# Two attention layers on one core: value batches sized to the score group, and softmax sums of layer 0 merged before they are summed over partitions

## The chip, the cores and the metric

The kernel runs on one core of a Trainium2 chip, in one launch. The metric is the device time of a run in microseconds; less is better. The core's engines run side by side and wait for each other through semaphores: TensorE (PE in the profile, its weight loads PEld), VectorE (DVE), ScalarE (ACT), GpSimd (POOL) and SyncE (SP, which issues transfers here).

## What is computed

The input x has 8 images of 64 channels and 64x64 positions, in 32-bit floats. Two self-attentions over the 4096 positions of each image follow each other:

```python
# layer 0
f = Wf @ x; g = Wg @ x            # 8 channels each
h = Wh @ x                        # 64 channels
beta = softmax(f.T @ g, axis=2)   # 4096 x 4096 for each image
x = x + h @ beta.T
# layer 1
xn = group_norm(x)                # 8 groups
q, k, v = split(w_qkv @ xn)       # 64 channels each
attn = softmax(q.T @ k / 8)
x = x + w_proj @ (attn @ v)
```

The kernel takes no maximum out of the softmax: it computes exponentials of the scores, the values weighted by them, and the sums of the exponentials, and multiplies by the reciprocal sums at the end. A general path for inputs whose sums leave a safe range stands behind a branch and isn't run here.

## The kernel before

An image's positions are kept as two halves of 2048 side by side on the partitions (64 channels of each half). The queries are worked on in 4 chunks of 512 columns of both halves (`NC`, `CW`), and for each chunk the keys in 16 steps t of 128 positions from each half p (`NT`). One *block* of scores in layer 0 is 128 keys by 512 queries: for one t there are four, (p, h) with p the half of the keys and h that of the queries. One block fills one PSUM bank. Images and layers follow each other as layer 0 of image 0, layer 0 of image 1, layer 1 of image 0, layer 0 of image 2, layer 1 of image 1 and so on. So there is one first stretch of layer 0 with two images (8 chunks) and six later ones of 4 chunks, each between stretches of layer 1.

TensorE's instructions are kept in the order in which the program makes them (`in_order`); those of the other engines are placed by a scheduler, within what `issue_after` says. All TensorE matmuls go through one helper, L137.

In a stretch of layer 0 the loop at L748 makes one *group* at a time. Eight PSUM banks are there: 1 to 6 for scores or lent to other work in pairs, and 0 and 7 (`outer`) as accumulators of the values, of which the one that is free at the moment takes a seventh block of scores. The group so has

- 7 blocks when the second accumulator is free (`closed == 0`) and no work wants it (`taken != BANK`),
- 6 otherwise,
- and 2 fewer when a pair of banks is lent (`taken == PAIR`) to a projection, a values product or the like, which `take` gives out by due steps.

After the group's scores, `scalar.activation` at L776 makes the exponentials, up to four banks at a time, into tiles `e` that hold the four blocks of one t (128x2048 floats; six such tiles, `ppool`). Then `ended` makes the due work and the *batch* of values: `weigh` multiplies values by finished exponentials of earlier groups into an accumulator (`acc`). `due_part` (L629) takes the batch from the list `ready`, whose entries are the two blocks of one (t, p). It counts in half blocks of the batch, 256 of an entry's 512 columns being one, so that an entry counts two, and takes up to 7 of them whatever the group holds; an entry that doesn't fit whole is cut in the middle. Blocks and half blocks balance, since one block of scores gives one half block to weigh.

For each t, VectorE adds the e tile into the chunk's `esum` (L662, 128x2048): esum has four parts, (p, h). At the chunk's end `finish` (L303) makes the rest in pieces with due steps: `sums` multiplies by ones, which adds over the partitions (four products, each in its own 32 columns of the array and its own 32 rows of the result), ScalarE copies the result to `zs`, four small transfers deal it over partitions as `zt`, `reciprocals` inverts it and sends it round through DRAM as `r`, and `result` multiplies the weighted values (`raw`) by it and adds the residual.

In layer 1 `finish` first merges the two p parts of esum on VectorE (L312, 128x1024), and the ones products take 256 columns each. In layer 0 there is no merge: the ones products take 512 columns each, one for every (h, p), and the two p parts are added later as 128x8 numbers (L345).

Of the kernel before, what the change touches and what calls it, by code (L numbers as in the profile page):

```python
# [9 lines left out]
F32 = mybir.dt.float32  # L10
# [9 lines left out]
CW = 512  # L20
P = 128
# [47 lines left out]
def fast_path(  # L69
# [19 lines left out]
    nc = tc.nc  # L89
    B, C, N = x.shape  # L90
# [11 lines left out]
    work = ctx.enter_context(tc.tile_pool(name="work", bufs=2))  # L102
    small = ctx.enter_context(tc.tile_pool(name="small", bufs=2))
# [89 lines left out]
    ones = const.tile([P, C], F32, name="ones")  # L193
# [18 lines left out]
    QP = 2 * CW // P  # L212
# [64 lines left out]
    class Attention:  # L277
# [25 lines left out]
        def finish(self, acc, esum, c, index):  # L303

            n = f"{self.name}_{c}"
            raw = work.tile([P, CW], F32, tag="raw", bufs=4, name=f"raw_{n}")
            copied = self.total(raw, acc)
            zt = small.tile([P, 2, QP], F32, tag="zt", bufs=5, name=f"zt_{n}")
            width = CW if self.kind == 0 else CW // 2
            if self.kind == 1:  # L310
                with tc.issue_after(copied.ins):
                    nc.vector.tensor_add(esum[:, 0], esum[:, 0], esum[:, 1])  # L312
            r = None

            def sums(spare):

                if spare is not None:
                    z = banks[:, spare, :]
                else:
                    z = pair()[:, 0, :]  # L320

                zs = work.tile([P, CW], F32, tag="zs", bufs=1, name=f"zs_{n}")[:, 0:width]
                for h in range(2):
                    for i in range(2):
                        row = 32 * (2 * h + i)
                        what = esum[:, i, h, :] if self.kind == 0 else esum[:, 0, h, ts(i, width)]
                        matmul(
                            z[row : row + 32, 0:width], ones[:, 0:32], what,
                            start=True, stop=True, tile_position=(0, row),
                        )  # L330
                nc.scalar.copy(zs, z[:, 0:width])  # L331
                for h in range(2):
                    for i in range(2):
                        row = 32 * (2 * h + i)
                        dst = zt[ts(h, C), i, :] if self.kind == 0 else zt[row : row + 32, 0, :]
                        nc.sync.dma_start(dst, zs[row : row + 1, :])

            def broadcast():
                nonlocal r
                r = work.tile([P, CW], F32, tag="r", name=f"r_{n}")  # L340

            def reciprocals():
                zh = zt[:, 0, :]
                if self.kind == 0:
                    nc.vector.tensor_add(zh, zh, zt[:, 1, :])  # L345
                rt = stash[:, ts(index, QP)]
                nc.vector.reciprocal(rt, zh)
                broadcast()
                dealt = recips[index]
                nc.sync.dma_start(dealt, rt)  # L350
                for h in range(2):
                    row = dealt[ts(h, C), :].rearrange("p e -> (p e)")
                    nc.sync.dma_start(r[ts(h, C), :], row.partition_broadcast(C))

            def at_once():

                broadcast()
                z = pair()[:, 0, :]
                for h in range(2):
                    matmul(z[ts(h, C), :], ones, esum[:, 0, h, :], start=True, stop=True)  # L360
                nc.vector.reciprocal(r, z)  # L361
                result()
                bounds(r, 1)

            def result():
                nc.vector.tensor_mul(raw, raw, r)  # L366
                self.residual(raw, c)

            if index == 2 * B * NC - 1:
                return (at_once,)  # L370
            return sums, reciprocals, result
# [219 lines left out]
    PAIR, BANK = 1, 2  # L591
# [33 lines left out]
    ready = []  # L625
    acc = esum = first = None
    added = None

    def due_part(ready):  # L629


        room, now_, left = 7, [], []
        for k, j, e, cols in ready:
            size = (cols.stop - cols.start) // (CW // 2)
            if seq[k][0].kind == 1 or room >= size:
                now_.append((k, j, e, cols))
                room -= size
            elif room == 1 and 0 < j < 2 * NT - 1:
                mid = (cols.start + cols.stop) // 2
                now_.append((k, j, e, slice(cols.start, mid)))  # L640
                left.append((k, j, e, slice(mid, cols.stop)))
                room = 0
            else:
                left.append((k, j, e, cols))
                room = 0
        return now_, left
# [60 lines left out]
    closed = 1  # L707
# [14 lines left out]
    while i < len(seq):  # L722
        at, c = seq[i]
        if at.kind == 1:
            for j in range(0, 2 * NT, 2):
                now = i * NT + j // 2
                due, taken = take(now)
                batch, left = ready, []
                t = j // 2
                new = []  # L730
                both_ps = [pair(), pair()]
                for p in range(2):
                    at.scores(both_ps[p], t, p, c)
                e = ppool.tile([P, 2, 2, CW], F32, tag="e", name=f"e_{at.name}_{c}_{t}")
                for p in range(2):
                    nc.scalar.activation(e[:, p], both_ps[p], AF.Exp, scale=at.scale)  # L736
                    new.append((i, j + p, e, slice(0, CW)))
                ended()
            i += 1
            continue  # L740

        last = next(k for k in range(i, len(seq) + 1) if k == len(seq) or seq[k][0].kind == 1)
        units = [
            (k, t, p, h)
            for k in range(i, last) for t in range(NT) for p in range(2) for h in range(2)
        ]
        u = 0
        while u < len(units):  # L748
            k, t = units[u][:2]
            now = k * NT + t  # L750
            due, taken = take(now + 1)
            batch, left = due_part(ready)
            free = outer[1]
            if batch:
                free = outer[(batch[-1][0] + 1) % 2]
                if seq[batch[-1][0]][0].kind == 1 or any(b[1] == 0 for b in batch):
                    closed = max(closed, 1)
            room = list(range(1, 7))
            if closed == 0 and taken != BANK:
                room = sorted(room + [free])  # L760
            if taken == PAIR:
                lent = 0 if room[-1] == 7 else 2
                room = [r for r in room if r not in (2 * lent + 1, 2 * lent + 2)]
            group = list(zip(units[u : u + len(room)], room))
            u += len(group)
            for (k, t, p, h), bank in group:
                seq[k][0].scores(banks[:, bank, :], t, p, h, seq[k][1])
            new = []
            while group:
                (k, t, p, h), bank = group[0]  # L770
                first_ = 2 * p + h
                n_ = min(4 - first_, len(group))
                at, c = seq[k]
                if first_ == 0:
                    e = ppool.tile([P, 2, 2, CW], F32, tag="e", name=f"e_{at.name}_{c}_{t}")
                nc.scalar.activation(  # L776
                    e.rearrange("k p h n -> k (p h) n")[:, first_ : first_ + n_, :],
                    banks[:, bank : bank + n_, :], AF.Exp, scale=at.scale,
                )
                new += [  # L780
                    (k, 2 * t + p, e, slice(0, CW)) for (k, t, p, h), _ in group[:n_] if h == 1
                ]
                group = group[n_:]
            ended()
            lent = None
        i = last
# [5 lines left out]
    bad_ps = banks[0:1, 0, 0:1]  # L792

    def bounds(recip, i):
        ok = work.tile(list(recip.shape), F32, tag="zs", bufs=1, name=f"ok_{i}")
        nc.vector.tensor_scalar(ok, recip, 1.0 / SUM_MAX, None, op0=ALU.is_ge)
        nc.vector.scalar_tensor_tensor(
            ok, recip, 1.0 / SUM_MIN, ok, op0=ALU.is_le, op1=ALU.mult
        )
        least = small.tile([P, 1], F32, tag="least", name=f"least_{i}")  # L800
        nc.vector.tensor_reduce(least, ok, axis=AX.X, op=ALU.min)
        nc.vector.tensor_scalar(bad[:, i : i + 1], least, -1.0, 1.0, op0=ALU.mult, op1=ALU.add)
# [395 lines left out]
```

## Time and profile before

| | |
|---|---|
| median time of 3 runs | 3106.06 us (3105.13 to 3106.15) |
| span of the profiled execution | 3104.1 us |
| TensorE, matmuls busy | 3063.5 us (99%) |
| VectorE busy | 2506.6 us (81%) |
| ScalarE busy | 2045.5 us (66%) |
| first stretch of layer 0 | 23 to 343 us |
| a later stretch of layer 0 | 958 to 1106 us |
| a stretch of layer 1 | 1106 to 1340 us |

The table's last three rows are from the times of the exponentials in the timeline. A matmul of 32-bit floats is two records in the trace (two for each product of values and of ones), one of scores in layer 0 is one record. In the timeline `fg_l` (or `kq_l` with 32*128) are layer 0's scores, `e_l,vt_l` (or `e_l,v_l` with 128*64) its batches, and `esum_l,ones` the ones products; the second number of a row is the time from its first record's start to its last one's end, so what a group occupies is better read from its start to the next group's start. A batch of six half blocks is 12 records of 512 columns; those that are cut have some of 256.

### The profile page before, as it was taken

How to read it: one execution, taken by the hardware profiler on the slowest of the kernel's cores; microseconds unless marked ns; L12 is line 12 of the kernel's file. 1: busy time of each engine (PE TensorE's matmuls, PEld its weight loads, DVE VectorE, ACT ScalarE, POOL GpSimd, SP SyncE). 2: the span in 40 equal slices, each digit the busy share in tenths (PEclk: the TensorE clock that was granted, in tenths of full speed). 3: DMA queues.
4: the chain of work that ended last, by engine and by line, in shares of the span. 5: the costliest groups of instructions: out<-in, count | busy, mean ns of one | idle time of the engine just before them, and what ended most of it. 6: DMA issues, size and time to landing. Idle time of an engine off the chain costs nothing.

```text
span 3104.1 us, 58905 instructions
## 1 busy us (share of the span) xinstructions
PE 3063.5 (99%) x25863; PEld 1122.5 (36%) x25863; DVE 2506.6 (81%) x1616; ACT 2045.5 (66%) x1976; POOL 16.7 (1%) x41
## 2 busy tenths in 40 slices
PE   7999999999999999999999999999999999999998
PEld 2333334333343333433334333343334333334433
DVE  6999876898768987689877997779977799776666
ACT  5788655786557865578555785558855587555554
POOL 2000000000000000000000000000000000000000
PEclk9999999999999999999999999999999999999999
DMA  3000010100101001010011000100001000000000
GB/s 84 22 8 11 18 39 15 32 1 15 39 21 26 1 15 39 22 25 1 15 39 25 21 1 19 42 19 21 1 25 35 19 8 2 14 22 15 10 13 12
DMA packets 61816, 63.16 MB, mean 20 GB/s; under 512 B 34944, under 2 KB 35024, under 8 KB 61552
## 3 DMA queue, kind: packets, MB, share of 16 engines
q1 hardware_dynamic: 60432, 59.16, 7.8%
q8 instruction: 204, 3.34, 0.5%
q14 instruction: 60, 0.49, 0.1%
q0 software_dynamic: 800, 0.15, 0.0%
q10 hardware_dynamic: 320, 0.01, 0.0%
HBM read 25.06 MB, written 8.65 MB: 11 GB/s over the span
## 4 chain that ended last, share of the span: by engine, by line
PE 96%; DVE 1%; ACT 1%; issue 1%; SPq 0%; DMA 0%; ACTq 0%; DVEq 0%
PE banks L137 96%; DVE esum_l L662 1%; ACT e_l L776 1%; SPq L432 0%; ACT e_l L736 0%; DMA w<-in_WgT_dram 0%; DMA x<-in_x_dram 0%; DVE vt_l L298 0%; DVE r_l L361 0%; DVE high_l L422 0%; DMA fg_l<-high_l 0%; ACTq L169 0%; DVE raw_l L366 0%; DVE esum_l L312 0%; ACT full_l L417 0%
## 5 line engine op out<-in xcount | busy, mean ns | idle before, releaser
L662 DVE TENSOR_TENSOR esum_l<-esum_l,e_l 128x2048 f32<-128x2048 f32 x896 | 2052.4, 2291 | 473.2 <-ACT e_l L736 414.5
L736 ACT ACTIVATE e_l<-banks 128x1024 f32<-128x1024 f32 x1024 | 992.8, 1021 | 802.8 <-PE banks L137 770.1
L137 PE MATMUL banks<-e_l,v_l 64*64 64x512 f32 (+1 forms) x8744 | 1098.5, 589 | 0.0
L776 ACT ACTIVATE e_l<-banks 128x2048 f32<-128x2048 f32 (+3 forms) x768 | 955.7, 1310 | 213.1 <-PE banks L137 207.9
L137 PE MATMUL banks<-kq_l 64*64 64x512 f32 (+1 forms) x8448 | 1010.2, 586 | 1.2 <-ACT e_l L776 1.1
L137 PE MATMUL banks<-e_l,vt_l 128*64 128x512 f32 (+1 forms) x3884 | 831.5, 567 | 0.0
L137 PEld LDWEIGHTS banks<-e_l,v_l 64*64 64x64 f32 (+1 forms) x8744 | 360.0, 133 | 576.0 <-issue 534.0
L137 PEld LDWEIGHTS banks<-kq_l 64*64 64x64 f32 (+1 forms) x8448 | 348.7, 134 | 579.3 <-issue 544.6
L137 PEld LDWEIGHTS banks<-e_l,vt_l 128*64 128x64 f32 x3884 | 254.3, 136 | 470.4 <-issue 457.0
L137 PE MATMUL banks<-fg_l 32*128 32x512 f32 x1792 | 220.2, 465 | 10.7 <-ACT e_l L776 5.7
L662 DVE TENSOR_TENSOR esum_l<-e_l,e_l 128x2048 f32<-128x2048 f32 x64 | 146.5, 2288 | 48.4 <-ACT e_l L736 35.9
L137 PEld LDWEIGHTS banks<-fg_l 32*128 32x128 f32 x1792 | 92.1, 183 | 219.4 <-ACT e_l L776 134.8
L137 PE MATMUL banks<-esum_l,ones 128*32 128x512 f32 (+2 forms) x508 | 55.2, 501 | 4.4 <-DVE esum_l L312 2.7
L568 DVE COPY raw_l<-banks 128x512 f32<-128x512 f32 x32 | 22.1, 692 | 31.3 <-PE banks L137 31.3
L366 DVE TENSOR_TENSOR raw_l<-raw_l,r_l 128x512 f32<-128x512 f32 x64 | 43.8, 684 | 0.0
L542 ACT ACTIVATE kq_l<-banks,qkb 128x512 f32<-128x512 f32 x64 | 40.6, 696 | 0.0
L312 DVE TENSOR_TENSOR esum_l<-esum_l 128x1024 f32<-128x1024 f32 x32 | 38.9, 1216 | 0.0
L137 PE MATMUL banks<-xn_l,wqk 64*64 64x512 f32 x256 | 33.4, 592 | 0.0
L331 ACT COPY zs_l<-banks 128x512 f32<-128x512 f32 (+1 forms) x63 | 30.9, 491 | 0.0
L137 PE MATMUL banks<-x,wfg 64*64 64x512 f32 x128 | 19.0, 640 | 9.7 <-DVE low L179 9.3
L137 PEld LDWEIGHTS banks<-wh,x 64*64 64x64 f32 x1024 | 22.0, 135 | 15.7 <-issue 13.3
L137 PEld LDWEIGHTS banks<-wvp,xn_l 64*64 64x64 f32 x1024 | 20.6, 134 | 16.8 <-issue 16.8
(89 smaller groups left out, 378.2 us busy)
## 6 DMA issues: line engine op xcount, KB each, us to landing
r_l<-recips SPq DMA_DIRECT2D x126, 128.0 KB, 2.9
fg_l<-high_l SPq DMA_DIRECT2D x224, 64.0 KB, 2.0
x<-in_x_dram SPq DMA_DIRECT2D x32, 256.0 KB, 5.2
kq_l<-kq_l SPq DMA_DIRECT2D x64, 128.0 KB, 2.3
out_dram<-raw_l SPq DMA_DIRECT2D x64, 128.0 KB, 2.4
kq_l<-high_l SPq DMA_DIRECT2D x32, 64.0 KB, 2.0
zt_l<-zs_l SPq DMA_DIRECT2D x128, 2.0 KB, 1.8
zt_l<-zs_l SPq DMA_DIRECT2D x124, 1.0 KB, 1.7
```

The lines of the kernel that those rows point to most:

```text
L137: in_order(nc.tensor.matmul(*args, **kwargs))
L312: nc.vector.tensor_add(esum[:, 0], esum[:, 0], esum[:, 1])
L331: nc.scalar.copy(zs, z[:, 0:width])
L366: nc.vector.tensor_mul(raw, raw, r)
L542: nc.scalar.activation(self.parts[:, h, cols], ps[:, h, :], AF.Identity, bias=k1["qkb"][:, h : h + 1],)
L568: nc.vector.tensor_copy(raw, acc[0])
L662: added = nc.vector.tensor_add(esum, first if t == 1 else esum, e).ins
L736: nc.scalar.activation(e[:, p], both_ps[p], AF.Exp, scale=at.scale)
L776: nc.scalar.activation(e.rearrange("k p h n -> k (p h) n")[:, first_ : first_ + n_, :], banks[:, bank : bank + n_, :], AF.Exp, scale=at.scale,
```

## The change

Three things are changed.

1. The size of a batch of values in layer 0 follows the size of the score group it stands behind: 7, 6, or two fewer, by the same conditions. It is meant to keep TensorE's and ScalarE's work per group in step, since ScalarE has as many blocks to exponentiate as the group holds while TensorE weighs the batch.
2. In layer 0, too, VectorE merges the two p parts of esum once per chunk, right after the chunk's last add.
3. With merged sums, the ones products of layer 0 take 256 columns in place of 512, the copy to `zs` is half as wide, and the small add in `reciprocals` goes. The buffers are changed to fit: `zs` has two, `zt` four of half the size, and the tile of the bounds check at the end moves from the buffer of `zs` to those of `raw`.

```diff
-            zt = small.tile([P, 2, QP], F32, tag="zt", bufs=5, name=f"zt_{n}")
-            width = CW if self.kind == 0 else CW // 2
-            if self.kind == 1:
-                with tc.issue_after(copied.ins):
-                    nc.vector.tensor_add(esum[:, 0], esum[:, 0], esum[:, 1])
+            zt = small.tile([P, QP], F32, tag="zt", bufs=4, name=f"zt_{n}")
+            width = CW // 2
+            with tc.issue_after(copied.ins if self.kind == 1 else added):
+                nc.vector.tensor_add(esum[:, 0], esum[:, 0], esum[:, 1])
...
-                zs = work.tile([P, CW], F32, tag="zs", bufs=1, name=f"zs_{n}")[:, 0:width]
+                zs = work.tile([P, width], F32, tag="zs", name=f"zs_{n}")
...
-                        what = esum[:, i, h, :] if self.kind == 0 else esum[:, 0, h, ts(i, width)]
                         matmul(
-                            z[row : row + 32, 0:width], ones[:, 0:32], what,
+                            z[row : row + 32, 0:width], ones[:, 0:32], esum[:, 0, h, ts(i, width)],
...
-                        dst = zt[ts(h, C), i, :] if self.kind == 0 else zt[row : row + 32, 0, :]
-                        nc.sync.dma_start(dst, zs[row : row + 1, :])
+                        nc.sync.dma_start(zt[row : row + 32, :], zs[row : row + 1, :])
...
-                zh = zt[:, 0, :]
-                if self.kind == 0:
-                    nc.vector.tensor_add(zh, zh, zt[:, 1, :])
                 rt = stash[:, ts(index, QP)]
-                nc.vector.reciprocal(rt, zh)
+                nc.vector.reciprocal(rt, zt)
...
-    def due_part(ready):
+    def due_part(ready, room):
-        room, now_, left = 7, [], []
+        now_, left = [], []
...
-            batch, left = due_part(ready)
+            wide = 7 if closed == 0 and taken != BANK else 6
+            batch, left = due_part(ready, wide - (2 if taken == PAIR else 0))
...
-        ok = work.tile(list(recip.shape), F32, tag="zs", bufs=1, name=f"ok_{i}")
+        ok = work.tile(list(recip.shape), F32, tag="raw", bufs=4, name=f"ok_{i}")
```

## The prediction

> **What bounds the kernel now.** I read the page's busy shares first, then the chain that ended last, then the costliest groups with shapes kept apart, then the timeline of TensorE and of VectorE in one layer 0 stretch.
>
> The page's first part and the start of its fourth:
>
> ```profile
> PE 3063.5 (99%) x25863; PEld 1122.5 (36%) x25863; DVE 2506.6 (81%) x1616; ACT 2045.5 (66%) x1976; POOL 16.7 (1%) x41
> ...
> PE 96%; DVE 1%; ACT 1%; issue 1%; SPq 0%; DMA 0%; ACTq 0%; DVEq 0%
> ```
>
> TensorE is the bound: matmuls are 96% of the chain. But "99% busy" doesn't say that it streams at its pace; that is read from start to start in TensorE's timeline, here around one chunk boundary of the second layer 0 stretch (columns: start us, us, engine, line, operation, count):
>
> ```profile
> 586.78 0.64 PE L137 MATMUL banks<-esum_l,ones 128*32 128x256 f32 x8
> 587.35 2.79 PE L137 MATMUL banks<-e_l,vt_l 128*64 128x512 f32 x12
> ...
> 627.90 1.06 PE L137 MATMUL banks<-esum_l,ones 128*32 128x512 f32 x8
> 628.90 3.23 PE L137 MATMUL banks<-e_l,vt_l 128*64 128x256 f32 x16
> 632.05 0.73 PE L137 MATMUL banks<-fg_l 32*128 32x512 f32 x6
> 632.72 2.80 PE L137 MATMUL banks<-e_l,vt_l 128*64 128x512 f32 x12
> 635.44 0.74 PE L137 MATMUL banks<-fg_l 32*128 32x512 f32 x7
> 636.11 2.79 PE L137 MATMUL banks<-e_l,vt_l 128*64 128x512 f32 x12
> 638.84 0.98 PE L137 MATMUL banks<-fg_l 32*128 32x512 f32 x7
> 639.75 3.23 PE L137 MATMUL banks<-e_l,vt_l 128*64 128x512 f32 x16
> 642.91 0.73 PE L137 MATMUL banks<-fg_l 32*128 32x512 f32 x7
> ```
>
> Three things are to be seen. The ones products of 512 columns occupy 628.90 - 627.90 = 1.00 us, those of 256 columns 587.35 - 586.78 = 0.57. A batch of six half blocks takes 635.44 - 632.72 = 2.72, of seven 642.91 - 639.75 = 3.16, also where it is cut into 256-column pieces (628.90 to 632.05 = 3.15), so cutting costs nothing. And seven scores take 0.67 (635.44 to 636.11) unless seven scores and a batch of only six stand before them: then 0.91 (638.84 to 639.75).
>
> That last 0.24 us is a wait for ScalarE: seven blocks need one 2048-column exponential and one of 1536, 1876 + 1453 ns = 3.33 us, while TensorE comes back to the same PSUM banks after 2.72 + 0.67. With a batch of seven it comes back after 3.83 and waits for nothing.
>
> VectorE is the second engine to watch, since layer 0 loads it fully. The groups with shapes kept apart:
>
> ```profile
> L662 DVE TENSOR_TENSOR esum_l<-esum_l,e_l 128x2048 f32<-128x2048 f32 x896 | 2052.4, 2291 | 473.2 <-ACT e_l L736 414.5 <-ACT e_l L776 16.1 <-DVE esum_l L662 0.9
> L312 DVE TENSOR_TENSOR esum_l<-esum_l 128x1024 f32<-128x1024 f32 x32 | 38.9, 1216 | 0.0
> ```
>
> VectorE's timeline (start us, us), and the second chunk of the third stretch by engine (length, then busy us of TensorE, its weight loads, VectorE and ScalarE):
>
> ```profile
> 987.98 11.87 DVE L662 TENSOR_TENSOR esum_l<-esum_l,e_l 128x2048 f32<-128x2048 f32 x5
> ...
> 993.00:1030.00 37.00, 37.00 (x217) 12.45 (x215) 35.55 (x16) 30.97 (x29) 0.00 (x0) 1.00 0.06 14
> ```
>
> Only 16.1 us of the adds' idle time is for layer 0's exponentials (L776). Five dependent adds take 11.87, so they start (11.87 - 2.29) / 4 = 2.395 apart; fifteen per chunk are 35.9 us, and a chunk lasts 37.
>
> **What the Trainium skill says.** "Perfetto Trace Analysis", Identifying the Most-Contended Engine, warns that matmul occupancy is a poor measure; the trace agrees, since the 0.24 us waits lie inside the 99%. "VectorE: DVE Perf Modes", The TRN2 errata, gives an fp32 tensor add as (N+151)/0.96 ns: 2291 for 2048 elements and 1224 for 1024; the trace has 2291 and 1216, and I use the trace. "TensorE: Matmul & The Clock Gate", Back-to-back issue gap, has a stream cost in proportion to its columns; the trace agrees in the difference, 1.00 - 0.57 = 0.43 us for half the columns.
>
> **The change part by part.** Counts for the changed kernel are those of its built order of instructions; it has 828 score or layer 1 groups and 828 batches, as before, so no overhead of a group is added.
>
> 1. *Ones products of 256 columns.* 32 chunks x 0.427 us (finer starts: 0.996 - 0.569) = 13.7 us off TensorE. It is on the bound everywhere, in layer 1 too, where the last chunk of each image's layer 0 has its products. The copy of sums on ScalarE falls from 595 to 383 ns, beside TensorE.
>
> 2. *Batches matched to the group.* The work is the same; only waits go. In the timeline before, seven scores after (seven scores, six half blocks) occur 46 times and cost 11.9 us over their 0.665, smaller batches between large groups in the first stretch cost another 5. Over 0.66 per group, a later layer 0 stretch (six of them, some 150 us each) loses 2.60: 0.67 on entering from layer 1, and eight waits of 0.20 to 0.29. In the built order three of those eight are left per stretch, with the entry: 0.67 + 0.21 + 0.25 + 0.29 = 1.42. Saved 1.2 x 6 = 7.1. The first stretch (two images, 20 to 345 us) loses 11.1, of which I find some 3.9 still there (start-up, and two groups of five after S7 V6): 7.2 saved. Where a projection or a values copy shares the group, five scores and five half blocks stand against 1876 + 601 ns of exponentials and 0.6 to 1.4 us of copies; TensorE has 2.30 + 0.63 to 1.02 + 0.66 there, so at most 0.3 us of wait each, some six times; I take it inside the 3.9.
>
> 3. *Merge on VectorE.* 32 adds of 1.216 plus a 0.10 gap, less the small add of 0.16 and 0.035 gap: +1.13 us a chunk. It isn't on the chain, as long as VectorE's lag finds room. The lag delays three users. The ones products stand 9.8 us or more after the chunk's last add (later stretches), so they don't wait. ScalarE needs a free e tile, of six: before, the exponentials of tile n+6 start at least 4.3 us after the add of tile n ended (chunks of a later stretch: 4.3, 5.7, 6.1, 8.4). I carry the adds forward, each starting at the later of its exponential's end and 2.396 after the one before: with the merges and a stretch 2.5 to 2.9 us shorter, the lag at a stretch's end grows from 1.8 to about 7.5 us and the room falls to 3.6, 3.0, 1.4, 2.2. Positive, so nothing waits; layer 1, where an add has 3.43 us, takes the lag back. Behind the merge are queued the next chunk's adds and, in layer 1's first steps, reciprocals and results, which no one is waiting for.
>
> 4. *First stretch.* Here VectorE also has projections, results and layer 1's normalisation. Carried forward in the same way, its lag in the sixth chunk rises from about 3 to 8 or 9 us and the room to 0 to 1.6. TensorE's first product of normalised columns (254.67) now comes 2.39 us after the columns are done (252.28); 5.3 us more lag gives a wait of about 3, plus half a us at the deviations before. I take 3.5 us lost, once; ends 0 and 10.
>
> 5. *Buffers* (sums copy twice, zt four times, the check's tile among the raw tiles): no new wait; their last users end many us earlier.
>
> Sum: 13.7 + 7.1 + 7.2 - 3.5 = 24.5. 3106.1 - 24.5 = 3081.6.
>
> **Rivals.**
> - *VectorE's extra work is free everywhere*: 3106.1 - 28.0 = 3078.1. For it: the ring of tiles absorbs lag. Against: slack of only 2.4 us at the normalised columns.
> - *The waits move instead of going.* The batch holds more half blocks back, and ScalarE then limits at other groups: only the ones products count, 3106.1 - 13.7 + 3.5 = 3095.9. For it: ScalarE needs 3.33 to 3.5 us of a 3.83 period. Against: 61 cases of (seven scores, seven half blocks, seven scores) lose 0.2 us in all.
> - *VectorE becomes the bound of layer 0* (slower). If my room is wrong by a few us, the exponentials wait for tiles and each merge is paid for in full, 32 x 1.13 = 36 us, with only the seven shortened ones products in layer 1 kept, 3.0: 3106.1 + 36 - 3 = 3139. For it: adds already fill 35.9 of 37 us. Against: all six tiles' room, 4.3 us at the worst, and it starts afresh in each stretch.
>
> **How the numbers follow.** Forecast 0.62, free merges 0.17, waits moved 0.15, VectorE bound 0.06. The predicted time is the forecast's. The range runs from 3077 (free, with a us for a wait that I left standing) to 3092 (first stretch at its dear end, or half of the waits moved). Faster 0.92: the first three cases and part of none other; same 0.03: VectorE bound in part, so that it eats the gain; slower 0.05.
>
> **What would show it.** Right: ones products of layer 0 at 0.57 from start to start; fewer 0.91 score groups, about three a stretch; VectorE's adds up to 7 us behind their exponentials at a stretch's end with no exponential waiting for them; a wait of some us before 250 at TensorE on xn. Wrong: ScalarE's exponentials (L771 in the new file) waiting for VectorE's adds, score groups still at 0.9 after full batches, or ones products waiting for the merge.

## The result, and the profile after

The changed kernel takes 3089.84 us (median of 4 runs, 3088.12 to 3090.6) against 3106.11 us: a ratio of 0.9947, 95% interval 0.993 to 0.9965. It is faster by 16.3 us, two thirds of the 24.5 that were forecast, and inside the range.

The page of the changed kernel, first part and start of the fourth:

```profile
PE 3043.7 (99%) x26071; PEld 1132.3 (37%) x26071; DVE 2538.6 (82%) x1616; ACT 2038.7 (66%) x1971; POOL 16.5 (1%) x41
...
PE 95%; DVE 3%; ACT 1%; issue 1%; SPq 1%; DMA 1%; ACTq 0%; DVEq 0%
```

TensorE is still the bound, but VectorE's share of the chain rose from 1% to 3%. TensorE's timeline shows what was bought, here in the second layer 0 stretch, at the same chunk boundary as before:

```profile
626.84 0.64 PE L137 MATMUL banks<-esum_l,ones 128*32 128x256 f32 x8
627.40 2.79 PE L137 MATMUL banks<-e_l,vt_l 128*64 128x512 f32 x12
630.13 0.73 PE L137 MATMUL banks<-fg_l 32*128 32x512 f32 x6
630.79 2.79 PE L137 MATMUL banks<-e_l,vt_l 128*64 128x512 f32 x12
633.52 0.73 PE L137 MATMUL banks<-fg_l 32*128 32x512 f32 x7
634.18 3.23 PE L137 MATMUL banks<-e_l,vt_l 128*64 128x512 f32 x16
637.34 0.73 PE L137 MATMUL banks<-fg_l 32*128 32x512 f32 x7
638.00 3.23 PE L137 MATMUL banks<-e_l,vt_l 128*64 128x256 f32 x16
```

The ones products occupy 0.56 us (627.40 - 626.84) where they had 1.00, and both groups of seven scores take 0.66 (637.34 to 638.00), since the batch ahead of each has as many half blocks as the group before that batch has blocks: six after six (630.13, 630.79), seven after seven (633.52, 634.18). The price is in the sixth chunk, near the end of the first stretch. TensorE's timeline there:

```profile
222.48 0.38 PE L137 MATMUL banks<-mv_l,gavg 128*128 128x1 f32 x2
222.80 2.37 PE L137 MATMUL banks<-e_l,v_l 128*64 128x256 f32 x12
225.10 0.73 PE L137 MATMUL banks<-kq_l 32*128 32x512 f32 x5
232.17 0.79 PE L137 MATMUL banks<-kq_l 32*128 32x512 f32 x2 [6.34 <-DVE mu_l L476]
232.90 5.07 PE L137 MATMUL banks<-e_l,v_l 128*64 128x512 f32 x12
```

and VectorE's:

```profile
223.71 1.22 DVE L311 TENSOR_TENSOR esum_l<-esum_l 128x1024 f32<-128x1024 f32 x1
224.85 2.28 DVE L656 TENSOR_TENSOR esum_l<-e_l,e_l 128x2048 f32<-128x2048 f32 x1
227.24 4.69 DVE L656 TENSOR_TENSOR esum_l<-esum_l,e_l 128x2048 f32<-128x2048 f32 x2
231.96 0.16 DVE L476 COPY mu_l<-banks 128x1 f32<-128x1 f32 x1
```

The mean's product (`mv_l,gavg`) writes into a lent pair of PSUM banks at 222.48. VectorE reads it out with a copy of 0.16 us, but the copy stands behind a merge and three adds, and is done at 232.12. The next group has five scores for other banks; the sixth needs the pair and starts 50 ns after the copy's end. TensorE stands idle for 6.34 us, and the batch behind it takes 5.00 us (237.90 - 232.90), not 2.73. The engines by stretches (length, busy us of TensorE, weight loads, VectorE, ScalarE and GpSimd, then TensorE's clock) say why:

```profile
227.00:230.00 3.00, 0.00 (x0) 0.00 (x0) 2.79 (x3) 0.10 (x1) 0.00 (x0) 1.00 0.00 0
230.00:233.00 3.00, 0.83 (x4) 0.39 (x6) 2.90 (x5) 0.00 (x0) 0.00 (x0) 0.62 0.00 0
233.00:236.00 3.00, 3.00 (x8) 0.90 (x10) 2.90 (x2) 1.88 (x1) 0.00 (x0) 0.50 0.00 0
236.00:239.00 3.00, 3.00 (x15) 0.96 (x13) 2.90 (x2) 0.52 (x1) 0.00 (x0) 0.75 0.00 0
```

VectorE is busy throughout while TensorE does nothing, and the clock granted to TensorE falls to 0.50 behind the idle time. The Trainium skill, "TensorE: Matmul & The Clock Gate", What's actually happening, tells of this: after an idle window of about 3.4 us the array runs at half its clock. The trace agrees: the clock falls between 230 and 233 us, about 5 us after the last score before the gap. Scores and batch together lose 7.1 + 2.3 = 9.4 us over their usual times.

Where the gain is, by the starts of layer 1's first scores in the timelines: the first stretch ends at 341.7 us, as before (341.6), and each of the six periods after it (a stretch of layer 1 and one of layer 0) takes 378.8 on the average where it took 381.7. 6 x 2.86 = 17.2 us is nearly all of the 17.7 between the spans of the two profiled executions (3104.1 and 3086.4); what the first stretch gained it lost at one copy.

### The profile page after: what moved, and what is told of

Its sections match the earlier page's. It is cut to its first block, busy times and chain, and to the rows that moved or that the text cites. A ratio compares the mean times of both kernels' runs of the same rounds, so it can differ in the third digit from the quotient of the medians.

```text
span 3086.4 us, 59347 instructions
## 1 busy us (share of the span) xinstructions
PE 3043.7 (99%) x26071; PEld 1132.3 (37%) x26071; DVE 2538.6 (82%) x1616; ACT 2038.7 (66%) x1971; POOL 16.5 (1%) x41
## 4 chain that ended last, share of the span: by engine, by line
PE 95%; DVE 3%; ACT 1%; issue 1%; SPq 1%; DMA 1%; ACTq 0%; DVEq 0%
PE banks L137 95%; DVE esum_l L656 2%; ACT e_l L730 0%; SPq L426 0%; ACT e_l L771 0%; DMA x<-in_x_dram 0%; DMA w<-in_WgT_dram 0%; DVE vt_l L298 0%; DVE high_l L416 0%; DVE esum_l L311 0%; SPq L145 0%; DVE r_l L355 0%; DMA fg_l<-high_l 0%; ACTq L169 0%; DVE high_l L413 0%
## 5 line engine op out<-in xcount | busy, mean ns | idle before, releaser
L656 DVE TENSOR_TENSOR esum_l<-esum_l,e_l 128x2048 f32<-128x2048 f32 x896 | 2052.3, 2291 | 455.9 <-ACT e_l L730 402.9
L137 PE MATMUL banks<-e_l,v_l 64*64 64x512 f32 (+2 forms) x8772 | 1100.9, 588 | 0.0
L137 PEld LDWEIGHTS banks<-e_l,vt_l 128*64 128x64 f32 x4064 | 267.5, 137 | 473.7 <-issue 453.7
L137 PE MATMUL banks<-fg_l 32*128 32x512 f32 x1792 | 211.0, 460 | 8.0 <-ACT e_l L771 4.4
L311 DVE TENSOR_TENSOR esum_l<-esum_l 128x1024 f32<-128x1024 f32 x64 | 78.1, 1220 | 0.9
L137 PE MATMUL banks<-esum_l,ones 128*32 128x256 f32 (+1 forms) x508 | 41.3, 393 | 4.5 <-DVE esum_l L311 2.8
L445 ACT COPY raw_l<-banks 128x512 f32<-128x512 f32 x32 | 19.0, 594 | 10.9 <-PE banks L137 10.8
```

Source lines behind the costliest of these rows:

```text
L137: in_order(nc.tensor.matmul(*args, **kwargs))
L445: nc.scalar.copy(raw, acc[0])
L656: added = nc.vector.tensor_add(esum, first if t == 1 else esum, e).ins
```

## The experiments

The question: is it the merges' load on VectorE that makes TensorE wait, or the new batches, or only the place of the mean's copy? And is the later stretches' room as narrow as forecast?

**The two halves apart.** Batches of up to seven again, the rest as changed:

```diff
-            batch, left = due_part(ready, wide - (2 if taken == PAIR else 0))
+            batch, left = due_part(ready, 7)
```

> The changed kernel with batches of up to 7 half blocks again, so only the merge and the narrow ones products are left of the change. Theory (the parts add up; VectorE's lag meets the mean's PSUM pair in the first stretch): ones products save 13.7 us, the waits of before stay at 25 us, and the merges alone put VectorE about 3 us further behind in the sixth chunk, which makes a wait of some 2.5 us after the mean's product: about 3095 us. Rival 1 (the wait in the first stretch comes from the new batches alone): no such wait, 3092.4. Rival 2 (it comes from the merges alone): the whole 9.4 us, 3102.

3097.42 us, ratio 0.9974 (0.9964 to 0.9984). And the kernel before with the new `due_part` and its call only:

> The kernel before with only the batches matched to the groups; no merge, ones products of 512 columns. Theory: the later stretches lose 1.2 us of waits each (7 in all), the first about 7, and a faster TensorE leaves VectorE some 4 us behind in the sixth chunk: wait after the mean's product of about 2.7 us, so about 3094.5 us. Rival 1 (the batches alone make the wait): 9.4 us of it, 3101. Rival 2 (the merges alone make it): no wait, 3092.

3095.77 us, ratio 0.9967 (0.9955 to 0.998). TensorE's timeline of the merges alone, then of the batches alone:

```profile
229.64 0.38 PE L137 MATMUL banks<-mv_l,gavg 128*128 128x1 f32 x2
...
236.21 0.50 PE L137 MATMUL banks<-kq_l 32*128 32x512 f32 x2 [2.59 <-DVE mu_l L476]
```

```profile
227.83 0.49 PE L137 MATMUL banks<-kq_l 32*128 32x512 f32 x2 [0.45 <-DVE mu_l L482]
...
235.34 0.49 PE L137 MATMUL banks<-kq_l 32*128 32x512 f32 x2 [0.58 <-DVE ve_l L491]
```

Each half alone makes the wait, but a short one, 2.6 (2.5 expected) and 0.5 + 0.6 us (2.7 expected in one wait); together they make 6.3. The times lie 2.4 and 1.3 us above the expected ones, nearest to the theory in both runs. The later periods are 380.0 and 380.6 on the average: savings of 1.7 and 1.1, together 2.8, where both have 2.9. So the parts add up in the later stretches and not in the first, where both push VectorE's lag the same way: the merges give it more to do, and the batches give it less time. At the end of the fifth chunk, just before the mean, VectorE's last add starts 3.0 us after its exponential's end in the kernel before, 3.9 with the batches alone, 5.4 with the merges alone and 8.6 with both.

**No merges in the first stretch:**

```diff
+            apart = self.kind == 0 and self.b < 2
+            width = CW if apart else CW // 2
+            if not apart:
+                with tc.issue_after(copied.ins if self.kind == 1 else added):
+                    nc.vector.tensor_add(esum[:, 0], esum[:, 0], esum[:, 1])
```

> The changed kernel, but the two images of the first stretch keep unmerged sums and ones products of 512 columns. Theory: the later stretches are as in the changed kernel; the first has the waits of its batches removed (7 us), no gain from ones products and a short wait of some 2.7 us for the mean: about 3085 us, 4 to 5 less than the changed kernel. Rival (the merge isn't what fills VectorE there): the first stretch is as long as in the changed kernel plus 3.4 us of wider ones products, 3093.

3084.04 us (3082.7 to 3085.8), ratio 0.9931 (0.9915 to 0.9948): faster than the changed kernel, although 8 of the ones products are wide again. The first stretch ends at 336.2, with the waits of the batches alone (0.5 for the mean, 0.6 for the variance) and the same lag of 3.9 us at the fifth chunk's end. The merges there cost more than they bring.

**The copies moved to ScalarE:**

```diff
-                nc.vector.tensor_copy(mu, ps[:, 0, 0:1])
+                nc.scalar.copy(mu, ps[:, 0, 0:1])
...
-                nc.vector.tensor_scalar_add(ve, ps[:, 0, 0:1], EPS)
+                nc.scalar.copy(ve, ps[:, 0, 0:1])
+                nc.vector.tensor_scalar_add(ve, ve, EPS)
```

> The changed kernel, with the mean and the variance read out of PSUM by ScalarE in place of VectorE; what is computed from them stays on VectorE. Theory (the 7 us wait is for the PSUM pair that VectorE's late copy holds, and the slow batch after it is the clock that fell): that wait and the slow batch, 9.4 us, go; the deviations' product then waits for v, which is still behind VectorE's adds, by some 3 us: about 3084 us. Rival (TensorE waits for VectorE's lag in any case, here or one step later): the wait moves to the deviations' product at its full length, about 3089.

3091.77 us, ratio 0.9957 (0.9941 to 0.9974): the rival was right, and its 3089 was still too low. TensorE's timeline:

```profile
226.08 0.74 PE L137 MATMUL banks<-kq_l 32*128 32x512 f32 x7
...
235.71 0.59 PE L137 MATMUL banks<-v_l,gavg 128*128 128x1 f32 x2 [5.04 <-DVE v_l L479]
236.23 4.07 PE L137 MATMUL banks<-e_l,v_l 128*64 128x512 f32 x12
```

The seven scores after the mean run through at 226.08. TensorE then stops at the next product that needs anything of VectorE: v is computed behind four late adds. I had allowed 3 us there; it was 5.0, a wait of 2.8 for the normalised columns followed, and the clock fell again. The PSUM pair was the place of the wait and not its cause. No run put these short steps ahead of the adds in VectorE's own order; whether that alone takes the waits away is open.

**More distance** (with the ScalarE copies): image 0's deviations 4 steps and its projections 6 to 3 steps later (not up to 8, as the expectation has it), its mean one step earlier,

```diff
-            at = [18, 21, 24] if self.b == 0 else [16, 20, 24]
+            at = [16, 20, 28] if self.b == 0 else [16, 20, 24]
...
-                s = 30 + 8 * c
+                s = (36 if self.b == 0 else 30) + (7 if self.b == 0 else 8) * c
```

> The changed kernel with the mean and the variance read by ScalarE, and image 0's deviations and projections of layer 1 due 4 to 8 steps later (steps 16, 20, 28, then 36 and every 7). Theory (what TensorE waits for is only that the normalisation's small VectorE steps stand behind VectorE's late adds, and enough distance hides it): the 9.4 us of the changed kernel go, 3080 to 3082 us. Rival (VectorE is the bound of the first stretch as a whole; distance moves the wait to e tiles or a later product): no gain over the changed kernel, 3088 or more.

3088.31 us, ratio 0.9945 (0.9929 to 0.9962), the rival's figure. The waits at the mean and the deviations are gone, and one for the normalised columns took their place: in TensorE's timeline

```profile
264.93 1.98 PE L137 MATMUL banks<-xn_l,wqk 64*64 64x512 f32 x8 [5.74 <-DVE xn_l L505]
```

These columns were still made only 3 steps ahead. So this distance was made 9 steps, with a second buffer for the columns; most of it comes from moving the products 6 to 3 steps further back:

```diff
-                    (s - 3, lambda c=c: normal(c), False),
+                    (s - (9 if self.b == 0 else 3), lambda c=c: normal(c), False),
...
+                s = (42 if self.b == 0 else 30) + (6 if self.b == 0 else 8) * c
```

> As the kernel with the later steps, but image 0's normalised columns are also made 9 steps, not 3, before their product (two buffers for them, one for the sums' copy). Theory (distance hides VectorE's lag): the 5.8 us wait and the slow batch after it, left in that kernel, go too: 3081 to 3083 us. Rival (VectorE as a whole is the bound from the fifth chunk on): ScalarE waits for e tiles instead, 3086 or more.

3084.56 us, ratio 0.9931 (0.9915 to 0.9948), between the two expectations. No product waits for the normalisation now, but ScalarE's timeline has

```profile
268.09 2.37 ACT L772 ACTIVATE e_l<-banks 128x2048 f32<-128x2048 f32 x2 [3.46 <-DVE esum_l L657]
```

an exponential waiting for VectorE to free an e tile. Distance hides part of the lag; the rest is VectorE's own work, for which the six tiles leave no room here (no run changed their number).

**The merge on GpSimd**, which is idle:

```diff
-                nc.vector.tensor_add(esum[:, 0], esum[:, 0], esum[:, 1])
+                (nc.vector if self.kind == 1 else nc.gpsimd).tensor_add(esum[:, 0], esum[:, 0], esum[:, 1])
```

> The changed kernel with layer 0's merges on GpSimd, which is idle. Theory (the merges' load on VectorE is the cause): VectorE's lag is that of the batches alone, the wait after the mean falls from 9 to about 2 us: 3080.6 to 3083 us, 7 or more less than the changed kernel. Rival (the two engines hinder each other, or the merge on GpSimd is late for the ones products): VectorE's adds get longer while it runs and the lag stays: 3086 or more.

3091.14 us, ratio 0.9954 (0.9937 to 0.997). The groups with shapes kept apart:

```profile
L656 DVE TENSOR_TENSOR esum_l<-esum_l,e_l 128x2048 f32<-128x2048 f32 x896 | 2109.5, 2354 | 436.7 <-ACT e_l L730 385.7 <-ACT e_l L771 5.6
...
L311 POOL TENSOR_TENSOR esum_l<-esum_l 128x1024 f32<-128x1024 f32 x32 | 131.4, 4106 | 2483.6 <-DVE esum_l L656 2245.2 <-DVE stash L341 238.4
```

The rival was right. A merge takes 4.1 us on GpSimd, and VectorE's 896 adds took 2052.3 us without it and 2109.5 with it: 57.2 / 32 = 1.8 us lost per merge, more than the 1.2 it would have cost on VectorE. The loss is all in the 29 of these adds that ran while a merge ran on GpSimd: they took 4.26 us on the average, the other 867 took 2.29 as before. (The first adds of the chunks, a group of their own in the trace, kept 2.30 beside a merge.) The wait after the mean is 8.0 us here. The Trainium skill, "GPSIMD Engine Reference", Specifications, says that GpSimd shares its SBUF interfaces with VectorE and contends with instructions of two SBUF inputs, as these adds are; these durations agree. Together with the ScalarE copies and the later steps:

> The merges on GpSimd together with the ScalarE reads and later steps. Theory: neither VectorE's load nor the distance is then short, all waits of the first stretch for VectorE are gone: about 3079 us. Rival (GpSimd hinders VectorE): 3084 or more.

3091.73 us, ratio 0.9954 (0.9938 to 0.9971): the rival again.

**A second merge in the later stretches**, to see how much room they have left:

```diff
                 nc.vector.tensor_add(esum[:, 0], esum[:, 0], esum[:, 1])
+                if self.kind == 0 and self.b > 1:
+                    nc.vector.tensor_add(esum[:, 1], esum[:, 0], esum[:, 1])
```

> The changed kernel with a second add of 128x1024 after each merge in the six later layer 0 stretches, into the part of the sums that is no longer read; it changes no output. Theory (a later stretch has 1.7 us of room for VectorE's lag at the worst place): 1.3 us more lag a chunk uses the room up in the third and fourth chunk, ScalarE then waits for e tiles, and each later stretch is about 1.3 us longer: 3096 to 3098. Rival 1 (there is more room than the trace's e tiles show): as the changed kernel, 3090. Rival 2 (VectorE is already the bound there): 4 x 1.3 us a stretch, 3121.

3110.77 us (3107.52 to 3117.3), ratio 1.0015 (1.0008 to 1.0022). The list of waits and, from the timeline, one of them:

```profile
ACT e_l L773 <- DVE esum_l L658: 19.5, 14, 2.8
```

```profile
699.40 4.20 ACT L773 ACTIVATE e_l<-banks 128x1024 f32<-128x1024 f32 x4 [2.45 <-DVE esum_l L658]
```

The room did run out, behind the third merge of a stretch (694.6); but a stretch lost 2.4 to 2.8 us at TensorE, not 1.3, and the time lies between the theory's and the second rival's. In two of the six the clock fell again and the next batch lost 1.3 us more, here with a mean clock of 0.60:

```profile
1464.00:1468.00 4.00, 4.00 (x12) 1.21 (x14) 3.79 (x3) 3.05 (x3) 0.00 (x0) 0.60 0.00 0
```

One add more per chunk eats the whole gain of the change. The size of the loss comes from a place that the count of 1.7 us of room left out. The first add of a chunk takes the chunk's first two tiles, so the first one is handed back only after the merge and that add. In the changed kernel's second stretch that add ends at 695.22 in the fourth chunk,

```profile
692.94 2.28 DVE L656 TENSOR_TENSOR esum_l<-e_l,e_l 128x2048 f32<-128x2048 f32 x1
```

and the exponential that takes the tile over starts at 696.16: 0.9 us of room (0.9 to 1.3 over the six stretches). Three second merges, 1.26 us each, are 3.8; less 0.9 that leaves 2.9, and ScalarE's waits in that stretch are 0.42 and 2.45.

**The version that follows:** no merges in the first five chunks, where they push the lag ahead of the normalisation; merges in the last three of the first stretch and in all later ones; the ScalarE copies and the later steps of image 0.

```diff
+            apart = self.kind == 0 and (self.b == 0 or (self.b == 1 and c == 0))
```

> The kernel without merges in the first stretch, but with merges again in its last three chunks, after the mean is taken, and with the ScalarE reads and later steps. Theory (only the merges ahead of the normalisation hurt): three ones products save 1.3 us and the two waits left there (1.8 us) go: 3081 to 3082.5 us. Rival (VectorE is short until the stretch's end): 3084 or more.

3081.69 us (3080.87 to 3082.24), ratio 0.9922 (0.9906 to 0.9939), the fastest of all and 8.15 us below the changed kernel. TensorE's timeline around the mean and the deviations:

```profile
223.75 0.38 PE L137 MATMUL banks<-mv_l,gavg 128*128 128x1 f32 x2
...
226.36 0.74 PE L137 MATMUL banks<-kq_l 32*128 32x512 f32 x7
...
242.21 0.38 PE L137 MATMUL banks<-v_l,gavg 128*128 128x1 f32 x2
...
260.18 1.09 PE L137 MATMUL banks<-xn_l,wqk 64*64 64x512 f32 x8
```

No row there, shown or left out, has an idle time for VectorE. How it stands with the others (from the timelines; profiled executions):

| kernel | median us | end of the first stretch | mean of the six later periods |
|---|---|---|---|
| before | 3106.1 | 341.6 | 381.7 |
| changed | 3089.8 | 341.7 | 378.8 |
| merges only | 3097.4 | 342.0 | 380.0 |
| batches only | 3095.8 | 337.1 | 380.6 |
| no merges in the first stretch | 3084.0 | 336.2 | 378.9 |
| merges from the sixth chunk on, ScalarE copies, later steps | 3081.7 | 334.3 | 378.8 |

## Why the prediction was right or wrong

- *Ones products*: right. The merges alone shorten a later period by 1.7 us = 4 x 0.43.
- *Batches*: right. A later stretch lost 2.6 us in score groups and loses some 1.4 now; what is left stands at the places named (on entry and three later).
- *Room in the later stretches*: right that nothing waits, with less to spare than I counted. VectorE's adds stand 7.6 us behind their exponentials at the second stretch's end (7.5 forecast). At the tiles that I counted, the room by chunks is 3.9, 3.0, 1.7, 2.6 (3.6, 3.0, 1.4, 2.2 forecast). But I left out the first tile of each chunk, which waits for the merge and the first add; there the fourth chunk has 0.9 to 1.3. That this held is in part luck; the second merge shows how near the end it was.
- *First stretch*: the mechanism, VectorE's lag holding up the normalisation, was right; its size and place were not. The step "I take 3.5 us lost, once" is the term that was mis-sized: it measured 9.4. I counted only products that need a result of VectorE, and with them found the normalised columns first. I missed that the mean's copy also holds a PSUM pair which the very next score group uses, so that the lag meets TensorE about 3 us behind the mean's product; the score group that waited isn't named in the step at all. And a wait of over 6 us has its own price in the clock, 2.3 us. The columns themselves then waited for nothing, since VectorE had caught up meanwhile.
- *The sum*: 24.5 forecast, 16.3 measured by the medians and 17.7 by the two profiled executions. In these the six later periods gained 17.2 where 17.3 was forecast (24 x 0.427 + 7.1), and the first stretch gained nothing where 6.7 was (7 x 0.427 + 7.2 - 3.5). Of the 6.8 missing, 5.9 is the term above, and 0.4 is a later start: the first score stands at 18.3 us in place of 17.9 (17.7 to 18.3 over all profiles). The 1.4 between the two measures is because the profiled execution of the changed kernel is the fastest of the four, 1.7 us under their median. A longer spell at half clock may be the reason: the two longest executions (3090.2 and 3090.6) have a mean clock of 0.994, the other two 0.995, and in the run with second merges, where this wait is 6.4 us, the clock from 222 to 240 is 0.72 on the average, here 0.81. But of the four executions only one has a trace, so this isn't shown.
- *The rivals*: free merges and moved waits are out, by the first stretch and by the score groups. VectorE as the bound of layer 0 was wrong as a whole, but one add more per chunk in the later stretches cost 20.9 us.

## What to carry to other kernels

An engine that is not the bound still has a schedule: before giving it work, list every place where the bound engine meets it, buffers that it is to hand back as well as results, and compare its lag with the distance at each of them. A buffer that an instruction holds together with another one comes back last; count the room there. Two changes that are each good alone can push the same lag and cost more together than apart; try them apart where the lag is largest. A wait moved away from one meeting place shows up at the next one, so take the load off ahead of the tight place before adding distance.

## What the runs showed of the hardware

An idle time of 6.3 us halved TensorE's clock, and the batch behind it took 5.00 us in place of 2.73. In the run with second merges TensorE's six idle times behind the third merge were 1.9 to 2.2 us, shorter than the window of about 3.4 that the page of the skill named above gives; two of them, 2.0 and 1.9, halved the clock too, and the two longest did not. So the length of one wait alone doesn't decide. Dependent adds of 2.29 us on VectorE start 2.40 apart, while an add behind an unrelated instruction starts up to 0.09 before that one's end: short instructions put between dependent adds cost less than their length. The add that follows the merge does so too: it starts at 224.85, before the merge's end at 224.93. Beside an add on GpSimd 29 of VectorE's adds took 4.26 us in place of 2.29, and 30 others 2.30.
